# A recurrent layer on one core: the decay of each step computed as a power of 1 + exp(v) on Pool, instead of as a power of two from the softplus

## The chip, the cores and the metric

The kernel runs as one program on one core of a Trainium2 chip. The metric is the time of one execution on the device, in microseconds (us). Before the change it is 4870.85 us, the median of 3 runs (4870.28 to 4872.86). Engines are named as in the profile: PE does matrix products, PEld loads their weights, DVE is the vector engine, ACT the one for activation functions, POOL (Pool) the general one, SP issues DMAs.

## The reference

The whole network has four layers, each an attention-like part and a feed-forward part. Only the first part of layer 0 is touched, a recurrence over 512 steps for 8 sequences. It cannot be computed in parallel over the steps, because the output of a step enters the projections of the next one:

```
def step(carry, inp):
    state, y_prev = carry
    xBC_t, dt_t, z_t = inp
    xBC = silu(xBC_t + y_prev @ W_rxbc.T)
    dtr = silu(dt_t + y_prev @ W_rdt.T)
    x_t, Bv, Cv = xBC[:, :256], xBC[:, 256:384], xBC[:, 384:]
    dt = softplus(dtr + dt_bias)
    dA = exp(dt * A)                                   # A = -exp(A_log), one for each of 4 heads
    state = state * dA + dt * x_h * Bv                 # 8 x 4 heads x 64 x 128
    y = (state * Cv).sum(-1) + D * x_h
    g = y * silu(z_t)
    yn = g * rsqrt(mean(g * g) + EPS) * norm_w
    return (state, yn), yn @ W_out.T
```

A head has 64 of the 256 inner channels. The step needs dt (how much of the new input enters the state) and dA (how much of the old state stays), one number of each for a head and a sequence.

## The kernel before, in words

`layer0` holds the loop. It is written with a manual schedule: each engine gets its instructions in the order of the program text, so the order of the lines is the order of the work on each engine. Engines wait for each other through semaphores.

The state is not updated in every step. `S` holds the state as of a multiple of eight steps (`Q = 8`), and the steps since then are kept as a list in `xw` (dt times x, already decayed to the present) beside their B rows in `h`. `held(t)` says which multiple is in use at step t, and `past` is the number of listed steps, 5 to 12. Every eight steps `update` folds the older entries into the next `S`, spread over the steps t mod 8 = 0 to 4 (its parts are called through `part(t, place)`). `spans` gives the columns of the ring of 16 entries that a step has to touch; with more than eight entries they are in two pieces.

Layout: 128 partitions are four groups of 32, with the 8 sequences in the first rows of each group for what is in rows, and the channels over the partitions for what is transposed. The DVE transpose works within blocks of 32 x 32, and carries data between the two. Before the change two heads stand in each partition group (the channels are in two halves of 128, and a half holds two heads), so dt is a tile of two columns, and dt and its decay need one transpose each.

A step goes like this, by the line numbers of the profile. PE squares the last step's output for its norm (L216, `pym`) and multiplies it with the recurrent weights (L216, `pag`). DVE sums the squares (L271, `ms`), Pool makes the power -1/2 (L274, `rh`), DVE scales the projections and adds the precomputed rows (L308, `a`), and ACT takes the silu (L314, `ar`), followed by a table load for the softplus (L211). DVE transposes (L316, `h`) and multiplies the listed B rows with C (L331, `cb`); PE sums these over the state dimension (L338, `G` in `pag`) and multiplies C (laid out by Pool in `Z`, L322) with the held state (L345, `py` in `pym`). ACT takes the softplus (L352, `dt`). DVE forms the weighted sum of the list (L358 `tmp`, L366 `R`), the exponent of the decay (L372), and Pool the power of two of it (L373, `da`). DVE turns dt, `py` and da (L255: `td`, `ty`, `dA`), and puts the output together: the share of the held state (L395, `y`), of the list (L386 and L401, `R`), both decayed (L408), and of the step itself (`M`, L383, L396, L406); their sum is `yh` (L409), on which PE waits for the next step. After that DVE decays the list (L418) for the next step.

Beside this the loop carries a second stream: the experts of layer 0's feed-forward part (`ffn.products` on PE, `ffn.activate` on ACT, `ffn.add` on DVE, a few in each step) and the projections of later steps (`aside`). `occupy` issues products of an identity matrix, whose results nobody reads, to fill PE where neither stream has work. `tables` loads ACT's table set, twice a step.

In the built program, where an instruction has to wait for two semaphores, an EventSemaphore instruction on the same engine stands ahead of it and waits for the first of them; the profile lists L308's, for instance, as 639 of 21 ns each.

Of the kernel before, what the change touches and what calls it, by code (L numbers as in the profile page):

```python
# [56 lines left out]
RW = 130  # L57
# [3 lines left out]
ASIDE = {5: 0, 7: 1, 13: 2, 15: 3, 9: 4}  # L61
LAG = 5


class Projections:
# [4 lines left out]
    def __init__(self, tc, ctx, K, I, dr, xn, xnT, B, T):  # L70
# [6 lines left out]
        self.WdtT = wp.tile([P, 8], F32, name="WdtT")  # L77
# [7 lines left out]
        with ExitStack() as c2:  # L85
# [9 lines left out]
            for c in range(2):  # L95
# [5 lines left out]
                self.dt(c, pz[:, 256:264])  # L101
                self.send(c, pz[:, 256:264])
# [19 lines left out]
    def send(self, c, ps):  # L122
        stg = self.stg.pop(c)
        self.nc.vector.tensor_copy(stg[:, :, P:RW], ps.rearrange("p (j c) -> p j c", j=4))
        self.pd[c] = self.dr.tile([4, TC, self.B, RW], F32, name=f"pd{c}")
        self.nc.sync.dma_start(out=self.pd[c].rearrange("j t b f -> (t b) j f"), in_=stg)
# [10 lines left out]
def layer0(tc, K, I, dr, xn, s_all, s_out, x, B, T):  # L137
# [12 lines left out]
    with ExitStack() as ctx:  # L150
# [18 lines left out]
        dtb = load("dtb", [P, 2])  # L169
        Dp = load("Dp", [P, 2, B])  # L170
        A2 = load("Al", [P, 2])
        selj = load("selj", [P, 2, P])
        nc.scalar.activation(A2, A2, AF.Exp)
        nc.vector.tensor_scalar(A2, A2, -1.0 / math.log(2.0), None, ALU.mult)
        two = wp.tile([P, 2], F32, name="two")
        nc.vector.memset(two, 2.0)
        for k in range(2):
            nc.vector.tensor_scalar(Wr[:, k], Wr[:, k], nw[:, k : k + 1], None, ALU.mult)
            nc.vector.tensor_scalar(WoT[:, k], WoT[:, k], nw[:, k : k + 1], None, ALU.mult)
        half = wp.tile([P, 1], F32, name="half")  # L180
# [21 lines left out]
        pdt, ring = paside[:, 256:264], [paside[:, 0:P], paside[:, P : 2 * P]]  # L202
# [58 lines left out]
        def pair(name):  # L261
            return wk.tile([P, 2], F32, name=name)
# [30 lines left out]
        def step(t, rt, zt):  # L293
# [26 lines left out]
            v, dt = pair("v"), pair("dt")  # L320
            nc.gpsimd.tensor_tensor(v, ar[:, P:RW], dtb, ALU.add)
            nc.gpsimd.tensor_copy(bass.AP(z9.tensor, z9.offset, [list(z9.ap[0]), [9, B]]), C)  # L322
            zd, xz, xd = small("zd"), small("xz"), small("xd")
            nc.gpsimd.tensor_tensor(zd, xw[:, :, :, SINCE[held(t) % 2]], zt, ALU.mult)
            nc.gpsimd.tensor_tensor(xz, x, zt, ALU.mult)
            nc.gpsimd.tensor_tensor(xd, xz, Dp, ALU.mult)
# [3 lines left out]
            for lo, hi in spans(t, t + 1):  # L330
# [5 lines left out]
                o += hi - lo  # L336
            for j in range(4):
# [14 lines left out]
            nc.scalar.activation(dt, v, AF.Softplus)  # L352
# [10 lines left out]

            def total(c):
                if past:
                    nc.vector.tensor_reduce(out=R[:, c, :], in_=tmp[:, c, :, 0:past], op=ALU.add, axis=AX.X)  # L366


            da, long = pair("da"), past > Q

            def power():
                tt_(da, dt, A2, ALU.mult)  # L372
                nc.gpsimd.tensor_tensor(da, two, da, ALU.pow)  # L373

            if long:
                power()
            total(0)
            total(1)
            if not long:
                power()  # L380
            td = turned(dt.unsqueeze(2).to_broadcast([P, 2, 32]), 2, "td")[:, :, 0:B]
            M = small("M")
            tt_(M, xz, G[:, :, past].unsqueeze(1).to_broadcast([P, 2, B]), ALU.mult)  # L383
            occupy(5 - given, pag[:, 384:])
            if past:
                tt_(R, R, zt, ALU.mult)  # L386
            part(t, "copies")
            if t % Q:
                ffn.activate(1 if t % TC in (9, 10) else 2 if t % TC in (3, 7, 11, 15) else 3)
            tables(SILU)  # L390
            nc.gpsimd.tensor_tensor(xw[:, :, :, s + 1], td, x, ALU.mult)
            part(t, "half 1")
            ty = turned(py.rearrange("p (c e) -> p c e", e=32), 2, "ty")
            y = small("y")
            tt_(y, zd, ty[:, :, 0:B], ALU.mult)  # L395
            tt_(M, M, td, ALU.mult)  # L396
            turn = lambda: turned(da.unsqueeze(2).to_broadcast([P, 2, 32]), 2, "dA")[:, :, 0:B]
            if long:
                dA = turn()
            if past:  # L400
                tt_(R, R, y, ALU.add)  # L401
            else:
                R = y
            if not long:
                dA = turn()
            tt_(M, M, xd, ALU.add)  # L406

            tt_(R, R, dA, ALU.mult)  # L408
            tt_(yh[:, :, :, t], R, M, ALU.add)  # L409

# [6 lines left out]
            for lo, hi in todo:  # L417
                tt_(xw[:, :, :, lo:hi], xw[:, :, :, lo:hi], dA.unsqueeze(3).to_broadcast([P, 2, B, hi - lo]), ALU.mult)  # L418
            if t % Q == 0:
                nc.vector.tensor_copy(xw[:, :, :, SINCE[n % 2]], dA)  # L420

        def update(q):
# [4 lines left out]
            das = st.tile([P, 2, 4, 4], F32, name="das")  # L427
            bs = st.tile([P, 2, P], F32, name="bs")
# [7 lines left out]

            def turn():
                xT = psU.tile([P, 2, 2, P], F32, name="xT", tag="u")
                both = psU.tile([P, 512], F32, name="bT", tag="u")
                bT = both[:, 0 : 2 * P].rearrange("p (r k) -> p r k", r=2)  # L440
                da = both[:, 2 * P : 2 * P + 4 * B].rearrange("p (c j b) -> p c j b", c=2, j=2)
# [1128 lines left out]
```

## Time and profile before

| | |
|---|---|
| median of 3 runs | 4870.85 us |
| profiled execution | 4871.46 us |
| its span | 4869.7 us |
| loop of layer 0, first to last L314 | 117.7 to 2902.1 us, 2784.4 us |
| busy in the loop: PE, DVE, ACT, POOL | 2694, 2111, 2221, 1384 us |
| granted PE clock in the loop | 1.00 of full |

The page of the profile has six parts. The second shows how the engines' load lies over the span, in 40 slices of about 122 us each, in tenths:

```profile
PE   6999999999999999999999997869999897999998
DVE  4777777777777777777777775747777325777771
ACT  2787788777787777887788773436666224666665
POOL 1455445444455444554544552620000345777782
```

The loop is the even stretch of some 23 slices from the second one on. PE looks full there, and DVE and ACT are busy for some three quarters of the time. None of these shares says what a step waits for, because PE's includes the filling products. That is read from the timeline and the chain of waits inside single steps. In a line of the timeline the columns are: start in us, duration in us, engine, line, operation, what is written and read, the shapes, the count, and in brackets how long the engine had been idle and what ended that. In a line of the groups of instructions they are: line, engine, operation, names, shapes, count, then busy time in all and the mean in ns, then idle time before and its releasers.

### The profile page before, as it was taken

Reading aid. Unit: us, or ns where it says so; the run is one execution under the profiler, and the core shown is the slowest. Engines: PE = TensorE matmul, PEld = TensorE weight load, DVE = VectorE, ACT = ScalarE, POOL = GpSimd, SP = SyncE. Lnnn points to the kernel's source line nnn. Section 1 sums busy time; section 2 is a strip of 40 time slices with the busy share of each in tenths; the row PEclk is TensorE's granted clock in tenths of the full one; section 3 lists DMA queues with packets and bytes.
Section 4 is the critical chain, followed back from the end, with each engine's and each line's share of the span. In section 5 each row is a group of like instructions: output and inputs, shape, how many; then the busy total and the mean of one; then the engine's idle time right before and its main releaser. Section 6 shows DMA issues by size and latency. Waiting matters only on the chain.

```text
span 4869.7 us, 193476 instructions
## 1 busy us (share of the span) xinstructions
PE 4555.9 (94%) x80433; PEld 3410.4 (70%) x80433; DVE 3393.6 (70%) x16561; ACT 3297.6 (68%) x6513; POOL 2241.9 (46%) x5416
## 2 busy tenths in 40 slices
PE   6999999999999999999999997869999897999998
PEld 5888888788877888788887885325555554666666
DVE  4777777777777777777777775747777325777771
ACT  2787788777787777887788773436666224666665
POOL 1455445444455444554544552620000345777782
PEclk6999999999999999999999998769999898999999
DMA  3000000000000000000000003100000510000000
GB/s 96 8 9 15 9 11 12 9 11 13 9 10 13 11 9 13 10 9 15 9 9 10 9 26 74 43 0 2 2 2 2 106 36 20 2 2 2 2 2 18
DMA packets 72706, 81.68 MB, mean 17 GB/s; under 512 B 8716, under 2 KB 55056, under 8 KB 71698
## 3 DMA queue, kind: packets, MB, share of 16 engines
q1 hardware_dynamic: 67116, 65.31, 5.5%
q8 instruction: 631, 10.34, 0.9%
q10 hardware_dynamic: 4710, 3.99, 0.3%
q14 instruction: 249, 2.04, 0.1%
HBM read 52.92 MB, written 16.36 MB: 14 GB/s over the span
## 4 chain that ended last, share of the span: by engine, by line
PE 54%; DVE 28%; POOL 7%; ACT 7%; issue 4%; DMA 1%; SPq 0%; DVEq 0%; ACTq 0%; POOLq 0%
PE pt L949 7%; PE ps_s L928 4%; PE pym L216 4%; POOL rh L274 4%; PE pym L221 3%; PE pag L338 3%; PE po L963 3%; PE pym L345 3%; PE ph L663 3%; PE us L468 3%; DVE a L308 2%; DVE R L366 2%; ACT ar L314 2%; DVE tmp L358 2%; DVE h L316 2%
## 5 line engine op out<-in xcount | busy, mean ns | idle before, releaser
L211 ACT ACT_TABLE_LOAD x1024 | 1313.8, 1283 | 17.7
L274 POOL TENSOR_TENSOR rh<-ms,half 128x1 f32<-128x1 f32 x512 | 281.3, 549 | 751.6 <-DVE ms L271 751.6
L345 PE MATMUL pym<-S,Z 128*8 128x64 f32 x32768 | 552.0, 219 | 0.2
L1247 POOL TENSOR_SCALAR gp<-toe,ng 128x207 f32<-128x207 f32 (+1 forms) x512 | 490.0, 965 | 111.2 <-DVE mn L936 75.9
L314 ACT ACTIVATE ar<-a 128x130 f32<-128x130 f32 x511 | 159.7, 313 | 534.4 <-DVE a L308 534.2
L949 PE MATMUL pt<-ident,sb 128*128 128x128 f32 x3328 | 498.7, 284 | 13.2 <-ACT pT L952 8.5
L949 PEld LDWEIGHTS pt<-ident,sb 128*128 128x128 f32 x3328 | 357.4, 141 | 209.6 <-ACT pT L954 78.6
L345 PEld LDWEIGHTS pym<-S,Z 128*8 128x8 f32 x32768 | 489.5, 90 | 0.9 <-POOL Z L322 0.8
L373 POOL TENSOR_TENSOR da<-two,da 128x2 f32<-128x2 f32 x512 | 356.8, 697 | 241.8 <-DVE da L372 241.8
L221 PE MATMUL pym<-ones,ident 128*128 128x128 f32 x3378 | 466.1, 277 | 0.0
L952 ACT COPY pT<-pt 128x512 f32<-128x512 f32 (+3 forms) x512 | 255.5, 499 | 245.0 <-PE pt L949 243.6
L221 PEld LDWEIGHTS pym<-ones,ident 128*128 128x128 f32 x3378 | 418.4, 192 | 0.7 <-DVE ms L271 0.4
L936 DVE CUSTOM_DVE_ANT_0 sb<-ps_s,gp 128x512 f32<-128x512 f32 x512 | 324.1, 685 | 102.8 <-PE ps_s L928 85.3
L216 PE MATMUL pag<-w_Wr,yh 128*8 128x130 f32 x8176 | 353.4, 278 | 0.0
L942 ACT ACTIVATE sb<-sb,mn 128x512 f32<-128x512 f32 (+3 forms) x512 | 330.6, 646 | 22.1 <-DVE mn L936 16.6
L358 DVE TENSOR_TENSOR tmp<-xw,pag 128x176 f32<-128x176 f32 (+2 forms) x635 | 159.8, 268 | 236.6 <-PE pag L338 236.6
L663 PE MATMUL ph<-xhT,ew 128*128 128x128 f32 x2048 | 315.8, 292 | 0.0
L308 DVE SCALAR_TENSOR_TENSOR a<-pag,rh,rows 128x130 f32<-128x130 f32 x511 | 180.6, 353 | 193.7 <-POOL rh L274 193.4
L485 ACT ACTIVATE Sd<-S,das 128x64 f32<-128x64 f32 x1008 | 306.1, 404 | 3.0
L673 ACT ACTIVATE hid<-ph,be 128x128 f32<-128x128 f32 x1024 | 305.8, 357 | 1.1 <-PE ph L663 1.1
L663 PEld LDWEIGHTS ph<-xhT,ew 128*128 128x128 f32 x2048 | 253.8, 191 | 70.0 <-issue 64.5
L646 PE MATMUL po<-ew,hid 128*128 128x128 f32 x2048 | 296.5, 288 | 6.0
(360 smaller groups left out, 10292.7 us busy)
## 6 DMA issues: line engine op xcount, KB each, us to landing
cB<-dc SPq DMA_DIRECT2D x16, 1024.0 KB
pd<-stg SPq DMA_DIRECT2D x32, 260.0 KB
rows<-pd SPq DMA_DIRECT2D x256, 32.5 KB
wu<-in_f_up_dram SPq DMA_DIRECT2D x9, 512.0 KB
wd<-in_f_down_dram SPq DMA_DIRECT2D x9, 512.0 KB
rd<-rv SPq DMA_DIRECT2D x1, 3304.0 KB
x<-in_u_dram SPq DMA_DIRECT2D x8, 256.0 KB
w<-in_f_w_dram SPq DMA_DIRECT2D x8, 256.0 KB
```

Source lines behind the costliest of these rows:

```text
L211: nc.scalar.preload_act_table_set(name)
L216: nc.tensor.matmul(out[32 * j : 32 * j + B, :], lhsT, rhs(j), start=(k == 0), stop=(k == 1))
L221: nc.tensor.matmul(where, ident, K["ones"], start=True, stop=True)
L274: nc.gpsimd.tensor_tensor(rh[:, t : t + 1], ms, half, ALU.pow)
L345: nc.tensor.matmul(py[32 * j : 32 * j + B, :], z9[:, B * b : B * b + B], Sq[b % 4][:, b // 4, :, 32 * j : 32 * j + 32], start=(i == 0), st ...
L373: nc.gpsimd.tensor_tensor(da, two, da, ALU.pow)
L485: nc.scalar.activation(Sd[:, 1, k, :], So[i][:, 1, k // 2, 64 * (k % 2) : 64 * (k % 2) + 64], AF.Copy, scale=das[:, 1, k, i : i + 1],)
L663: self.nc.tensor.matmul(self.ph[:, f, :], self.w[n][0][:, f * P : (f + 1) * P], self.xhT[:, i * P : (i + 1) * P], start=True, stop=True)
L936: nc.vector.tensor_tensor_reduce(out=sb[:, 0:L], in0=ps[:, g, 0:L], in1=bias[g], scale=1.0, scalar=3.0e38, op0=ALU.add, op1=ALU.min, accum ...
L942: nc.scalar.activation(sb[:, 0:L], sb[:, 0:L], AF.Exp, scale=-1.0, bias=mn)
L949: nc.tensor.transpose(pt[:, j * P : (j + 1) * P], sb[:, j * P : (j + 1) * P], self.ident)
L1247: nc.gpsimd.tensor_scalar(t[:, k0:k1], toe[:, h, o : o + k1 - k0], gates[b][:, i, h : h + 1], None, ALU.mult)
```

## The change

In the reference dA = exp(A softplus(v)) with v = dtr + dt_bias. Since softplus(v) = ln(1 + exp(v)), this is (1 + exp(v)) to the power A. The change computes it in that form. v is capped at 40 in the exponential; beyond that, the exponent is scaled by v/40 instead (`Acap`, `ad`).

- Decay: Pool computes min(v, 40), then Euler's number to that power (`base` holds it), plus one, and then the power `ad`, four dependent instructions from `ar` on. The softplus for dt stays on ACT and takes the bias itself. dt and the decay go into the two columns of one tile `dd`, which one transpose turns.
- Layout: each of the four partition groups holds one head. The channels are reordered in `layout` (`by_head`), so a half holds 32 channels of each head, dt has one column instead of two, and the rows of the projections have 129 columns for 130 (`RW`).
- Order: Z's copy, xz and the two small instructions for `ad` go to DVE, ahead of `tmp`. `za` (gate times decay), the product of M with dt and its sum with xd go to Pool, behind the transpose. y is multiplied with `za` once, in place of three products on DVE. In steps with `past` above 8 the transpose stands between the two reduces; else there is one reduce for both halves.
- The update of S every eight steps takes its decays through `decays`, a Pool product with a 0/1 mask `firsts`, and one product on PE, instead of two on PE with `selj`.
- ACT's ReLUs of the experts follow the table `RELUS` by t mod 8, and one filling product less is issued behind the held state's products.

```diff
-RW = 130
+RW = 129
+CAP = 40.0
+RELUS = [2, 1, 1, 1, 2, 4, 4, 3]
...
-            v, dt = pair("v"), pair("dt")
-            nc.gpsimd.tensor_tensor(v, ar[:, P:RW], dtb, ALU.add)
-            nc.gpsimd.tensor_copy(bass.AP(z9.tensor, z9.offset, [list(z9.ap[0]), [9, B]]), C)
-            zd, xz, xd = small("zd"), small("xz"), small("xd")
-            nc.gpsimd.tensor_tensor(zd, xw[:, :, :, SINCE[held(t) % 2]], zt, ALU.mult)
-            nc.gpsimd.tensor_tensor(xz, x, zt, ALU.mult)
-            nc.gpsimd.tensor_tensor(xd, xz, Dp, ALU.mult)
+            d, ad = ar[:, P:RW], one_("ad")
+            dd = wk.tile([P, 2], F32, name="dd")
+            e, w = one_("e"), one_("w")
+            nc.gpsimd.tensor_scalar(e, d, dtb, CAP, ALU.add, ALU.min)
+            nc.gpsimd.tensor_tensor(e, base, e, ALU.pow)
+            nc.gpsimd.tensor_tensor(e, e, one, ALU.add)
...
+            nc.vector.tensor_copy(bass.AP(z9.tensor, z9.offset, [list(z9.ap[0]), [9, B]]), C)
+            nc.vector.tensor_scalar(w, d, dtb, Acap, ALU.add, ALU.mult)
+            xz, xd = small("xz"), small("xd")
+            tt_(xz, x, zt, ALU.mult)
+            nc.vector.tensor_scalar(ad, w, A, None, ALU.min)
+            nc.gpsimd.tensor_tensor(dd[:, 1:2], e, ad, ALU.pow)
...
-            nc.scalar.activation(dt, v, AF.Softplus)
+            nc.scalar.activation(dd[:, 0:1], d, AF.Softplus, bias=dtb)
...
-            def power():
-                tt_(da, dt, A2, ALU.mult)
-                nc.gpsimd.tensor_tensor(da, two, da, ALU.pow)
...
+            M = small("M")
+            own = lambda: tt_(M, xz, both(G[:, :, past]), ALU.mult)
+            nc.gpsimd.tensor_tensor(xd, xz, Dp, ALU.mult)
+            turn = lambda: turned(dd.unsqueeze(2).to_broadcast([P, 2, 32]), 2, "td")
+            if past > Q:
+                nc.vector.tensor_reduce(out=R[:, 0, :], in_=tmp[:, 0, :, 0:past], op=ALU.add, axis=AX.X)
+                own()
+                turns = turn()
+                nc.vector.tensor_reduce(out=R[:, 1, :], in_=tmp[:, 1, :, 0:past], op=ALU.add, axis=AX.X)
+            else:
...
+                    nc.vector.tensor_reduce(out=R, in_=tmp[:, :, :, 0:past], op=ALU.add, axis=AX.X)
+                own()
+                turns = turn()
+            td, dA = both(turns[:, 0, 0:B]), turns[:, 1, 0:B]
+            occupy(4 - given, pag[:, 384:])
...
-            if t % Q:
-                ffn.activate(1 if t % TC in (9, 10) else 2 if t % TC in (3, 7, 11, 15) else 3)
+            ffn.activate(RELUS[t % Q])
...
+            za = small("za")
+            nc.gpsimd.tensor_tensor(za, zt, both(dA), ALU.mult)
+            nc.gpsimd.tensor_tensor(M, M, td, ALU.mult)
+            nc.gpsimd.tensor_tensor(M, M, xd, ALU.add)
             nc.gpsimd.tensor_tensor(xw[:, :, :, s + 1], td, x, ALU.mult)
...
-            tt_(y, zd, ty[:, :, 0:B], ALU.mult)
-            tt_(M, M, td, ALU.mult)
...
-            tt_(M, M, xd, ALU.add)
-            tt_(R, R, dA, ALU.mult)
-            tt_(yh[:, :, :, t], R, M, ALU.add)
+            tt_(y, xw[:, :, :, SINCE[held(t) % 2]], ty[:, :, 0:B], ALU.mult)
+            if past:
+                tt_(y, y, R, ALU.add)
+            tt_(y, y, za, ALU.mult)
+            tt_(yh[:, :, :, t], y, M, ALU.add)
...
+            def spread():
+                nc.gpsimd.tensor_tensor(
+                    decays, xw[:, 0, :, SINCE[q % 2]].unsqueeze(1).to_broadcast([P, 4, B]),
+                    firsts.unsqueeze(2).to_broadcast([P, 4, B]), ALU.mult,
+                )
...
-                for j in range(2):
-                    nc.tensor.matmul(
-                        da[:, :, j, :], selj[:, j, :], xw[:, :, :, SINCE[q % 2]], start=True, stop=True
-                    )
+                nc.tensor.matmul(da, K["ones"], decays, start=True, stop=True)
```

## The prediction

> **What bounds the kernel now.** I read the page first, then the chain of waits inside one step of the layer 0 loop, then the timeline of that step, then the same places over all steps. The page gives a span of 4869.7 us. The loop of 512 steps lies from the first L314 at 117.7 us to the last at 2902.1 us: 2784.4 us, 5.44 us a step. Nothing in the diff touches what comes after the loop. The timeline of one step (L314 starts at 1502.40; rows between are left out):
>
> ```profile
> 1502.40 0.31 ACT L314 ACTIVATE ar<-a 128x130 f32<-128x130 f32 x1 [1.43 <-DVE a L308]
> ...
> 1502.79 0.20 POOL L321 TENSOR_TENSOR v<-ar,w_dtb 128x2 f32<-128x2 f32 x1 [0.81 <-ACT ar L314]
> ...
> 1503.74 0.26 DVE L358 TENSOR_TENSOR tmp<-xw,pag 128x96 f32<-128x96 f32 x1 [0.43 <-PE pag L338]
> ...
> 1504.03 0.20 ACT L352 ACTIVATE dt<-v 128x2 f32<-128x2 f32 x1
> 1504.03 0.31 DVE L366 TENSOR_REDUCE R<-tmp 128x8 f32<-128x48 f32 x2
> ...
> 1504.51 0.70 POOL L373 TENSOR_TENSOR da<-two,da 128x2 f32<-128x2 f32 x1 [0.46 <-DVE da L372]
> ...
> 1504.56 0.17 DVE L386 TENSOR_TENSOR R<-R,z 128x16 f32<-128x16 f32 x1
> 1504.65 0.24 DVE L255 STREAM_TRANSPOSE ty<-pym 128x64 f32<-128x64 f32 x1
> 1504.92 0.17 DVE L395 TENSOR_TENSOR y<-zd,ty 128x16 f32<-128x16 f32 x1
> ...
> 1505.24 0.25 DVE L255 STREAM_TRANSPOSE dA<-da 128x64 f32<-128x64 f32 x1
> ...
> 1505.52 0.17 DVE L408 TENSOR_TENSOR R<-R,dA 128x16 f32<-128x16 f32 x1
> 1505.73 0.19 DVE L409 TENSOR_TENSOR yh<-R,M 128x16 f32<-128x16 f32 x1
> ```
>
> PE is busy 94% of the span, but much of that is the identity products that only fill time. The chain of waits runs L314, h, cb, PE L338, tmp, R, then DVE instruction after DVE instruction up to yh (L409), then PE, ms, rh, a (L308) and the next L314. From yh's start to the next L314 it is 1.96 to 1.99 us and nothing in the change lies on it. So **a step moves by as much as the start of yh moves against its own L314.** Call that distance Y, and count all times below from L314's start. Over all steps the trace has Y = 3.32 (t mod 8 = 5, 6), 3.36 (7), 3.45 (0), 3.55 (1 to 3), 3.58 (4): mean 3.46.
>
> What decides Y now: softplus (ACT, 1.63 to 1.83, right behind the 1.28 us table load), then DVE's da, then the Pool power of 0.70, 2.11 to 2.81, then dA's transpose and two dependent sums. DVE itself has almost no hole from 1.63 on.
>
> **What the change does to it.**
>
> *The decay leaves the softplus.* New Pool chain from ar: e (tensor_scalar 128x1), base^e, e+1, e^ad. Start 0.39, where v starts now. A dependent Pool instruction begins 0.08 after its predecessor's end (xz ends 1503.747, xd starts 1503.825). The power of one element has a row, the plus one is nearest to v's 0.195. The tensor_scalar has no small row. The groups kept apart by shape give
>
> ```profile
> L274 POOL TENSOR_TENSOR rh<-ms,half 128x1 f32<-128x1 f32 x512 | 281.3, 549 | 751.6 <-DVE ms L271 751.6
> L1247 POOL TENSOR_SCALAR gp<-toe,ng 128x286 f32<-128x286 f32 x256 | 270.4, 1064 | 57.7 <-DVE mn L936 57.7
> L1247 POOL TENSOR_SCALAR gp<-toe,ng 128x207 f32<-128x207 f32 x256 | 219.6, 866 | 53.5 <-issue 23.3 <-DVE mn L936 18.3 <-DVE ng L1208 11.1
> ```
>
> The medians of the two L1247 forms are 813 and 1009 ns, so 2.48 ns an element and 0.30 us at none. Below, v's 0.195 (a plain sum) bounds it; above, 0.30 + 0.195 = 0.50. I take **0.30**, since it comes from the same opcode with the same kind of operand. Then e 0.39 to 0.69, base^e 0.77 to 1.32, plus one 1.40 to 1.59, e^ad 1.67 to 2.22. DVE sees a Pool result 0.03 later (da's end to dA): **both are turned at T = 2.25**, where dA's transpose started at 2.83 to 3.04 before. Softplus is done at 1.83 as now and does not decide. This is the one new wait on DVE: behind it on that engine stand ty, y and all that leads to yh (in long steps the second reduce too), and PE's next products wait for yh.
>
> *DVE's row after T.* Two transposes follow each other by 0.16 (td to M now). So ty at T+0.16, lasting 0.24; y 0.03 behind its end, at T+0.43, 0.175 long; the sum with R 0.035 behind that, T+0.64 to T+0.82. The last two wait for DVE and Pool. The built program puts the DVE wait into an EventSemaphore of its own ahead of the instruction (three more a step on DVE). What that costs shows where it is there now, in layer 1 (timeline of DVE):
>
> ```profile
> 3122.28 1.24 DVE L807 TENSOR_SCALAR cp<-cp,ar,k 128x512 f32<-128x512 f32 x1 [0.46 <-ACT cp L806]
> 3123.62 0.69 DVE L810 TENSOR_TENSOR cp<-cp,pw 128x512 f32<-128x512 f32 x1
> ```
>
> L807 ends at 3123.51 and L810 starts 0.104 later (0.039, the semaphore instruction's 0.021, 0.044) instead of 0.034. So y*za runs from T+0.92 to T+1.10 and yh starts at **T+1.20**. In the long steps (t mod 8 = 1 to 4, over eight past values) the second reduce stands between the transposes: 0.15 more, T+1.35.
>
> *The sums on Pool* are cover, not path: za starts 0.08 behind the transposes' end, T+0.32; M*td 0.18 later; M+xd waits for it, T+0.81 to T+1.03; seen at T+1.06, ahead of y*za's end by only 0.04. xw follows, over before L419. If a Pool product were 0.1 us longer, M would decide.
>
> *Moved onto DVE ahead of tmp:* Z's copy, w, xz, ad, about 0.1 each. They fit into the 0.43 hole between cb and tmp, and tmp still waits for PE L338; Z is ready about when Pool had it (0.95 against 0.99). Were the hole gone, tmp could slip 0.1 before R's end would reach T. *Gone from DVE:* da, R*z, M*td, M+xd, one transpose, one reduce in short steps. Worth nothing alone: DVE now waits for T.
>
> *The rest costs nothing:* the long decay of S (0.62 on Pool) still runs between rh and e, with 0.2 us to spare; decays (128x32) runs between xw and rh; ACT has the ReLUs moved to the steps without the four L493 copies, and its second table load ends by 4.5 where the next L314 comes at 5.3; 478 of 2193 filling products go, all in front of PE's wait for yh; no DMA of the loop moves, rows and pd carry one column less in 130.
>
> **Sum.** With T = 2.25, Y becomes 3.45 in short steps and 3.60 in long ones. Against the trace: +0.13, +0.13, +0.09, 0.00, +0.05 three times, +0.02: 0.52 in eight steps, 0.065 a step, times 512 = **33 us slower**. The profiled execution took 4871.46 us (1.8 outside its span), the median shown is 4870.85: 4904.
>
> **Two rules against the trace.** The Trainium skill, *SBUF — State Buffer*, "Who interferes with whom": a DVE instruction with two SBUF inputs is locked out by a Pool instruction that reads SBUF[...]. Here R*z (L386, two SBUF inputs) starts 0.05 us into the 0.70 us power and takes its usual 0.17; only an instruction that starts within some 0.03 us of a Pool product loses anything (y, L395: 0.23 instead of 0.175 where xw on Pool starts just ahead of it). By the row the overlap costs nothing, by the rule Z's copy or y would sit out a power or a product: 0.1 to 0.3 us a step, 50 to 150 us. I take the row. *GPSIMD Engine Reference*, "Engine selection", speaks against moving two-input products to Pool (about twice the time). The row is 0.22 against 0.175. By the rule M would be ready at T+1.45 rather than T+1.06, another 0.25 a step, 128 us.
>
> **Rivals.**
> 1. *Forecast, 0.53*: the Pool chain sets T at about 2.25 and two semaphore instructions follow; 4904, own range 4880 to 4945.
> 2. *Faster, 0.28*: the tensor_scalar costs what a plain sum does. T = 2.15, Y falls by 0.04 on average, 4851. It decides from a price under 0.235, where the 0.065 is used up. For it: the fit is drawn from 207 elements down to one. Against: two forms and the 512 elements of L585 (1.57 us) lie on one line. If the semaphore instructions also slid under the running instruction (2 x 0.07), it would be 4833 with the larger price.
> 3. *Contention, 0.12*: the lock of the rule, about 5000. For it: y's 0.23. Against: L386.
> 4. *PE's clock, 0.07*: fewer filling products and 0.3 us more idling in front of yh lower the granted clock, now 1.00 over the whole loop; a tenth of the 2 us of PE work on the chain would be 0.2 a step, 4970.
>
> **How the numbers follow.** Time 4904. The low end takes in rival 2 and part of its second half, 4840; the high end takes the upper price only in part (0.50 would give +0.265 a step, 5006) and most of 4: 4975. A measurement of this kernel tells 0.2% (10 us) from no change. Faster: rival 2 but for its small cases, and a few of 1: 0.28. Within: 0.07. Slower: 0.65.
>
> **What would show it.** e's row on Pool at 0.30 and the start of the two-column transpose at 2.25 after L323 (the new number of L314); a gap of 0.10 in front of y*za and of yh; M+xd on Pool ending just before y*za. If e is under 0.24, or those gaps are 0.03, the sign turns. If the distance from yh to the next L323 changes, my claim that nothing else moves is wrong.

## The result, and the profile after

| | before | after |
|---|---|---|
| median | 4870.57 us (4868.89 to 4872.86, 4 runs) | 4916.23 us (4915.33 to 4929.06, 4 runs) |
| profiled execution, its span | 4871.46, 4869.7 us | 4929.06, 4926.9 us |
| loop, first to last silu (L314, now L323) | 2784.4 us | 2828.7 us |

The ratio is 1.010 (95% interval 1.0082 to 1.0117): the kernel became 46 us slower. The profiled execution is the slowest of the four; some 12 us of its excess lie behind the loop, 10 of them in layers 2 and 3, which the change doesn't touch, and the other three runs, at 4915 to 4916, are shorter by about as much. The loop's own 44 us, and its start 1 us later, make up 45 of the 46.

The second part of the page, three of its rows after the change (each digit the busy share of a fortieth of the span, in tenths; PEclk the granted TensorE clock):

```profile
PE   6988888888888888888888897869999897999998
...
POOL 1666666666666666666666662630000355767782
PEclk6999999999999999999999998769999898999999
```

PE went from nine tenths to eight in the loop, because the filling products went; Pool went from four or five to six; the clock stays at nine and more, and in the loop it is 1.00 as before. Rival 4, a lower clock, fell with this row.

The fourth part, the chain of work that ended last, by engine and by line:

```profile
PE 35%; DVE 25%; POOL 25%; issue 8%; ACT 6%; DMA 1%; DVEq 0%; SPq 0%; ACTq 0%; POOLq 0%
PE pt L955 7%; POOL rh L283 6%; POOL dd L351 5%; PE ps_s L934 4%; POOL e L334 4%; DVE a L317 4%; PE pym L221 3%; ACT ar L323 3%; PE po L969 3%; DVE td L260 2%; POOL e L333 2%; DVE yh L410 2%; DVE y L409 2%; DVE xw L419 2%; PE py L1122 2%
```

Before, the first row was:

```profile
PE 54%; DVE 28%; POOL 7%; ACT 7%; issue 4%; DMA 1%; SPq 0%; DVEq 0%; ACTq 0%; POOLq 0%
```

Pool's new instructions, e and dd, are on the chain now, and so is the transpose behind them. The power no longer waits for ACT, and hardly for DVE, but DVE waits for it.

The timeline of one step with t mod 8 = 6 (start in us, duration, engine, line, operation, names; in brackets the idle time before and what ended it). Its silu starts at 1568.90:

```profile
1568.90 0.31 ACT L323 ACTIVATE ar<-a 128x129 f32<-128x129 f32 x1 [1.70 <-DVE a L317]
...
1569.31 0.29 POOL L333 TENSOR_SCALAR e<-ar,w_dtb 128x1 f32<-128x1 f32 x1 [0.83 <-ACT ar L323]
...
1569.69 0.56 POOL L334 TENSOR_TENSOR e<-base,e 128x1 f32<-128x1 f32 x1
...
1570.59 0.55 POOL L351 TENSOR_TENSOR dd<-e,ad 128x1 f32<-128x1 f32 x1
...
1571.17 0.24 DVE L260 STREAM_TRANSPOSE td<-dd 128x64 f32<-128x64 f32 x1 [0.32 <-POOL dd L351]
1571.34 0.21 DVE L260 STREAM_TRANSPOSE ty<-pym 128x64 f32<-128x64 f32 x1
...
1571.59 0.18 DVE L406 TENSOR_TENSOR y<-xw,ty 128x16 f32<-128x16 f32 x1
...
1571.80 0.18 DVE L408 TENSOR_TENSOR y<-y,R 128x16 f32<-128x16 f32 x1
...
1571.98 0.22 POOL L400 TENSOR_TENSOR M<-M,xd 128x16 f32<-128x16 f32 x1
1572.08 0.17 DVE L409 TENSOR_TENSOR y<-y,za 128x16 f32<-128x16 f32 x1
...
1572.36 0.19 DVE L410 TENSOR_TENSOR yh<-y,M 128x16 f32<-128x16 f32 x1
```

Four Pool instructions (the third, e+1, lies between the rows shown) run one behind the other from 0.41 to 2.24 after the silu. DVE stands idle for 0.32 until the last has ended, and turns at 2.27. From there to yh it is 1.19. In the step shown before, dA's transpose came much later (1505.24, 2.84 after its silu), but only 0.49 lay between it and yh. So the decay is ready 0.57 earlier and yh still starts 0.13 later: what was done while DVE waited for the decay (turning `py`, forming `y`, adding `R`, multiplying M) now stands behind that wait.

The groups of Pool's instructions kept apart by shape (busy time in all, mean ns of one, idle time before and its releasers):

```profile
L334 POOL TENSOR_TENSOR e<-base,e 128x1 f32<-128x1 f32 x512 | 286.0, 559 | 42.6
...
L351 POOL TENSOR_TENSOR dd<-e,ad 128x1 f32<-128x1 f32 x512 | 280.3, 548 | 42.3 <-DVE tmp L373 2.0 <-POOL e L335 0.5 <-DVE ad L350 0.4
...
L333 POOL TENSOR_SCALAR e<-ar,w_dtb 128x1 f32<-128x1 f32 x512 | 149.5, 292 | 281.9 <-ACT ar L323 281.9
...
L335 POOL TENSOR_TENSOR e<-e,ones 128x1 f32<-128x1 f32 x512 | 97.3, 190 | 40.2
```

292 ns for the tensor_scalar against 190 for the plain sum is the price on which the prediction hung its sign. The idle time of 42 us over 512 steps, 0.08 each, in front of the dependent instructions is the gap that the prediction took from xz and xd.

### The profile page after: what moved, and what is told of

Same layout as the page of the kernel before. It is cut to its first block, busy times and chain, and to the rows that moved or that the text cites. A ratio compares the mean times of both kernels' runs of the same rounds, so it can differ in the third digit from the quotient of the medians.

```text
span 4926.9 us, 193651 instructions
## 1 busy us (share of the span) xinstructions
PE 4406.9 (89%) x79351; PEld 3282.5 (67%) x79351; DVE 3473.6 (71%) x15792; ACT 3346.8 (68%) x6513; POOL 2623.5 (53%) x6503
## 3 DMA queue, kind: packets, MB, share of 16 engines
q14 instruction: 267, 2.19, 0.2%
## 4 chain that ended last, share of the span: by engine, by line
PE 35%; DVE 25%; POOL 25%; issue 8%; ACT 6%; DMA 1%; DVEq 0%; SPq 0%; ACTq 0%; POOLq 0%
PE pt L955 7%; POOL rh L283 6%; POOL dd L351 5%; PE ps_s L934 4%; POOL e L334 4%; DVE a L317 4%; PE pym L221 3%; ACT ar L323 3%; PE po L969 3%; DVE td L260 2%; POOL e L333 2%; DVE yh L410 2%; DVE y L409 2%; DVE xw L419 2%; PE py L1122 2%
## 5 line engine op out<-in xcount | busy, mean ns | idle before, releaser
L323 ACT ACTIVATE ar<-a 128x129 f32<-128x129 f32 x511 | 159.7, 312 | 521.3 <-DVE a L317 521.1
L221 PE MATMUL pym<-yh 128*8 128x8 f32 x8192 | 231.7, 219 | 223.0 <-DVE yh L410 222.7
L226 PE MATMUL pym<-ones,ident 128*128 128x128 f32 x2942 | 417.6, 277 | 0.0
L221 PEld LDWEIGHTS pym<-yh 128*8 128x8 f32 x8192 | 173.5, 154 | 361.8 <-DVE yh L410 357.6
L226 PEld LDWEIGHTS pym<-ones,ident 128*128 128x128 f32 x2942 | 369.7, 192 | 0.4 <-DVE ms L280 0.4
L221 PE MATMUL pag<-w_Wr,yh 128*8 128x129 f32 x8176 | 352.7, 277 | 0.0
L317 DVE SCALAR_TENSOR_TENSOR a<-pag,rh,rows 128x129 f32<-128x129 f32 x511 | 180.6, 353 | 197.9 <-POOL rh L283 195.3
L334 POOL TENSOR_TENSOR e<-base,e 128x1 f32<-128x1 f32 x512 | 286.0, 559 | 42.6
L351 POOL TENSOR_TENSOR dd<-e,ad 128x1 f32<-128x1 f32 x512 | 280.3, 548 | 42.3 <-DVE tmp L373 2.0
```

Of the source, the lines that this page charges most:

```text
L221: nc.tensor.matmul(out[32 * j : 32 * j + B, :], lhsT, rhs(j), start=(k == 0), stop=(k == 1))
L226: nc.tensor.matmul(where, ident, K["ones"], start=True, stop=True)
L317: stt_(a, pa, rh[:, t - 1 : t], rt, ALU.mult, ALU.add)
L334: nc.gpsimd.tensor_tensor(e, base, e, ALU.pow)
L351: nc.gpsimd.tensor_tensor(dd[:, 1:2], e, ad, ALU.pow)
```

## The experiments

Y is, as in the prediction, the start of yh counted from the step's own silu, and T the start of the two-column transpose; both are medians by t mod 8 without the first 16 steps, averaged over the eight where one number is given. Short steps are those with t mod 8 = 0 and 5 to 7, long ones those with 1 to 4. A change of Y by 0.02 is worth 10 us. My theory: the loss is the price of e, plus a row behind T that is longer by two waits for two semaphores, with M on Pool only just hidden. Against it stood that DVE and Pool get in each other's way (the lock), that the shifted filling products and ReLUs cost the time, and that the layout itself is at fault.

| run | time, us | ratio to before (95%) | mean Y, us | step, us |
|---|---|---|---|---|
| before | 4870.57 | | 3.460 | 5.443 |
| after | 4916.23 | 1.010 (1.0082 to 1.0117) | 3.544 | 5.518 |
| e1: plain sum for e | 4882.84 | 1.0026 (1.0017 to 1.0035) | 3.473 | 5.448 |
| e2: M's sums on DVE | 4888.99 | 1.0040 (1.0023 to 1.0057) | 3.470 | 5.451 |
| e3: all three sums on DVE | 4913.66 | 1.0086 (1.0068 to 1.0104) | 3.519 | 5.497 |
| e4: layout alone | 4846.54 | 0.9948 (0.993 to 0.9965) | 3.391 | 5.389 |
| e5: `py` turned first | 4894.06 | 1.0049 (1.0033 to 1.0064) | 3.509 | 5.486 |
| e6: one more Pool product | 4935.2 | 1.0119 (1.0091 to 1.0147) | 3.572 | 5.548 |
| e7: old filling and ReLUs | 4918.64 | 1.0096 (1.0074 to 1.0118) | 3.551 | 5.527 |
| e8: no cap, row reordered | 4786.72 | 0.9820 (0.9799 to 0.9842) | 3.268 | 5.276 |
| e9: e8's row, with the cap | 4836.73 | 0.9936 (0.9914 to 0.9958) | 3.367 | 5.372 |

The times before in the sessions were 4868.7 (e1 to e4), 4871.66 (e5 to e8) and 4867.55 us (e9). All of e1 to e9 start from the changed kernel.

### e1: what the tensor_scalar costs

```diff
-            nc.gpsimd.tensor_scalar(e, d, dtb, CAP, ALU.add, ALU.min)
+            nc.gpsimd.tensor_tensor(e, d, dtb, ALU.add)
```

It leaves out the cap of v at 40 in the exponential.

> The changed kernel, with e formed by a plain Pool sum (v = d + dtb) instead of the tensor_scalar; the cap at 40 is left out. Theory (the Pool chain sets the start T of the two-column transpose): e takes 0.195 instead of 0.29, T goes from 2.27 to about 2.18, the step loses 0.09, 512 steps lose 48 us: about 4868, level with the kernel before. Rival (something else holds the transpose, softplus or DVE's own row): no change, 4916.

e took 0.190 and started 0.02 earlier (0.390), which alone would bring everything behind it 0.12 earlier, but T moved only from 2.276 to 2.201: by 0.11 to 0.13 where t mod 8 is 5 to 7, by 0.03 to 0.07 in the other steps. Why not further, its group on Pool shows:

```profile
L351 POOL TENSOR_TENSOR dd<-e,ad 128x1 f32<-128x1 f32 x512 | 280.8, 549 | 70.0 <-DVE ad L350 29.7 <-DVE tmp L373 3.5
L334 POOL TENSOR_TENSOR e<-base,e 128x1 f32<-128x1 f32 x512 | 280.7, 548 | 40.1
```

The idle time before the last power rose from 42.3 to 70.0 us, and 29.7 of it are now ended by DVE's `ad`, which the changed kernel's row names with 0.4. A wait that nothing had shown stood right behind the one removed. Y fell by 0.071, 36 us; the times differ by 33. The term is real and large, but not the whole loss: against before, 0.26% remain.

### e2: M's two sums back on DVE

```diff
-            nc.gpsimd.tensor_tensor(M, M, td, ALU.mult)
-            nc.gpsimd.tensor_tensor(M, M, xd, ALU.add)
...
             tt_(y, xw[:, :, :, SINCE[held(t) % 2]], ty[:, :, 0:B], ALU.mult)
+            tt_(M, M, td, ALU.mult)
             if past:
                 tt_(y, y, R, ALU.add)
+            tt_(M, M, xd, ALU.add)
             tt_(y, y, za, ALU.mult)
```

> The changed kernel, with the two sums of M (times td, plus xd) back on DVE, between y, the sum with R and the product with za. yh then waits for DVE alone, without a semaphore instruction ahead of it. Theory (each semaphore instruction that waits for the instruction just before it costs 0.07, and the gaps between dependent DVE instructions have room for independent ones): the gap in front of yh falls from 0.10 to 0.03, 36 us less, about 4880. Rival (two more DVE instructions on the row cost what they last, 0.09 each): 4916 or more, up to 5000.

Two more instructions on the engine that leads to yh made the kernel 0.6% faster. The timeline of DVE in the step corresponding to the one above (silu at 1548.62):

```profile
1551.30 0.18 DVE L404 TENSOR_TENSOR y<-xw,ty 128x16 f32<-128x16 f32 x1
1551.40 0.17 DVE L405 TENSOR_TENSOR M<-M,td 128x16 f32<-128x16 f32 x1
1551.52 0.17 DVE L407 TENSOR_TENSOR y<-y,R 128x16 f32<-128x16 f32 x1
1551.67 0.17 DVE L408 TENSOR_TENSOR M<-M,xd 128x16 f32<-128x16 f32 x1
1551.80 0.17 DVE L409 TENSOR_TENSOR y<-y,za 128x16 f32<-128x16 f32 x1
1552.01 0.19 DVE L410 TENSOR_TENSOR yh<-y,M 128x16 f32<-128x16 f32 x1
```

From y to y*za it takes 0.50, against 0.49 in the changed kernel without the two in between. An instruction that does not depend on the one ahead of it starts some 0.08 before that one's recorded end, as M's product with td does here (M's sum with xd, which has a semaphore of Pool to wait for, only 0.02), so the links of a chain of dependent sums leave room for one such instruction each. What is gained is behind y*za: yh starts 0.04 after its end (1551.97) instead of 0.11, because it no longer waits for Pool. That is the price of the second semaphore, 0.07 a step, 36 us; mean Y fell by 0.074, and the times differ by 27. It is not that Pool was late: in the changed kernel the gap ahead of y*za is the same 0.104, though za was done 0.25 and more before y+R ended. Nor did the program lose an EventSemaphore instruction: yh's stands ahead of M's sum with xd now, where the chain has room for it.

The Trainium skill, *GPSIMD Engine Reference*, "Engine selection", speaks against two-input sums on Pool for their duration, about twice that on DVE. Here they last 0.22 against 0.17, 1.3 times as long, and as long as they are hidden that duration is not what was paid: the wait at the meeting point was.

### e3: all sums behind the transpose on DVE

Besides e2's edit, `za` goes to DVE:

```diff
-            nc.gpsimd.tensor_tensor(za, zt, both(dA), ALU.mult)
...
             tt_(y, xw[:, :, :, SINCE[held(t) % 2]], ty[:, :, 0:B], ALU.mult)
+            tt_(za, zt, both(dA), ALU.mult)
+            tt_(M, M, td, ALU.mult)
```

> As e2_m_on_dve, with za on DVE too, so none of the sums behind the transpose is on Pool (xd and the product for the list stay there). The product with za then has no semaphore instruction (0.07 less), but three independent instructions stand between y and the sum with R, one too many for the gap (0.06 more). Theory: level with e2 within 30 us, 4880 to 4910. If Pool products held DVE up through the shared access to the memory, this one would be clearly the fastest of the two, below 4860.

With only one Pool product left beside DVE's row the kernel was no faster than e2 but slower by 0.5%. The row in the step with t mod 8 = 6:

```profile
1565.57 0.18 DVE L403 TENSOR_TENSOR y<-xw,ty 128x16 f32<-128x16 f32 x1
...
1565.83 0.17 DVE L407 TENSOR_TENSOR y<-y,R 128x16 f32<-128x16 f32 x1
1566.02 0.17 DVE L408 TENSOR_TENSOR M<-M,xd 128x16 f32<-128x16 f32 x1
1566.11 0.17 DVE L409 TENSOR_TENSOR y<-y,za 128x16 f32<-128x16 f32 x1
```

From y to y+R it takes 0.26 where e2 has 0.22, since two instructions stand in one link, where there is room for one. That is the whole difference between the two in mean Y (0.049). The 0.07 that the expectation counted for the semaphore ahead of y*za did not come: from y+R to y*za it is 0.28 in both, because M's sum with xd, which still waits for Pool, now starts only 0.02 behind y+R's end. In e8, where xd is on DVE too, it is 0.21.

Rival 3 is the Trainium skill's rule (*SBUF — State Buffer*, "Who interferes with whom": a DVE instruction with two SBUF inputs contends with a Pool instruction that reads SBUF, and the lock is exclusive). e3 alone can't rule it out, since the fuller link could hide a gain; the durations can. The traces have the lock, but it is short. A DVE sum of 128x16 that starts up to 0.07 behind the start of a Pool product of that size ends 0.243 to 0.249 after the Pool product's start, whenever in that time it began (the prediction had put the reach at 0.03): y in the long steps of the changed kernel (0.182 to 0.205, 0.066 to 0.043 behind M's product with td), y before (up to 0.234) and here where t mod 8 = 0 (0.228), R+y in e4. One that starts later than that (y in short steps, 0.18), or just ahead of the Pool product (y+R, 0.175), is not longer. So a Pool product holds DVE up as if for the first 0.07 of its 0.22 and no longer, at most 0.06 of delay. In the changed kernel that is 0.03 in the worst step, where rival 3 counted some 0.25 in each. It fell.

### e4: the layout without the new order

Layer 0's step in the old order, with the old softplus and power of two, on one head to a partition group; what stays of the change is `by_head`, `RW` and `decays`:

```diff
-            nc.gpsimd.tensor_scalar(e, d, dtb, CAP, ALU.add, ALU.min)
...
-            nc.gpsimd.tensor_tensor(dd[:, 1:2], e, ad, ALU.pow)
+            nc.gpsimd.tensor_tensor(v, ar[:, P:RW], dtb, ALU.add)
...
+                tt_(da, dt, A2, ALU.mult)
+                nc.gpsimd.tensor_tensor(da, two, da, ALU.pow)
```

> One head a partition group, as in the changed kernel, but the step itself in the order of the kernel before: softplus, exponent on DVE, power of two on Pool, two transposes, sums on DVE. Theory: the power has one element instead of two (0.55 instead of 0.70) and the transposes are half as wide; DVE's row is nearly full, so only 0.07 to 0.12 of the 0.15 reaches yh: 36 to 61 us below the kernel before, 4810 to 4835. Rival (DVE's row alone bounds the step): 4870.

The layout alone is a gain of 0.5%, smaller than expected. What became shorter is the power, on one column instead of two, in the group of Pool's instructions:

```profile
L379 POOL TENSOR_TENSOR da<-two,da 128x1 f32<-128x1 f32 x512 | 292.6, 572 | 240.3 <-DVE da L378 240.3
```

572 ns where before had 697; dt's and dA's transposes fell from 0.24 to 0.205. In long steps yh came 0.07 to 0.12 earlier. The shortfall is in the short ones, on DVE: dA's transpose starts where it did (2.836 against 2.832), though the power ended 0.10 earlier, and R+y (0.175 before) took 0.19 to 0.226, because xw on Pool starts just ahead of it. Of the 0.069 that Y gained, 0.015 was lost again behind yh, half of it where t mod 16 = 9 and the period stayed at 5.63. So the change as a whole is two things of opposite sign: 24 us won by the layout, 70 lost by the new decay and the new order together.

### e5: the held state's share turned ahead of the decay

```diff
+            ty = turned(py.rearrange("p (c e) -> p c e", e=32), 2, "ty")
+            turns = turn()
```

in place of the two in the opposite order, and both reduces ahead of them.

> The changed kernel with one change of order on DVE: ty (which needs only PE's py, ready at about 2.2 in short steps and 2.35 in long ones) is turned ahead of dt and decay, and both reduces stand ahead of the transposes. M stays on Pool. Theory (the sums of M on Pool are hidden by no more than 0.04, as the prediction had it): y starts 0.17 to 0.3 earlier, but the two-column transpose moves back to 2.36 and 2.51, M follows it by 1.06, and yh now waits for Pool: 3.42 and 3.58, some 0.04 a step, about 4896. Rival (M is well hidden, DVE's chain behind ty decides): 0.17 a step, 4830.

The time came out within 2 us of the expectation. The timeline of DVE's row and Pool's M at t mod 8 = 6 (silu at 1555.40):

```profile
1557.63 0.25 DVE L260 STREAM_TRANSPOSE ty<-pym 128x64 f32<-128x64 f32 x1 [0.27 <-PE pym L360]
...
1558.44 0.17 DVE L406 TENSOR_TENSOR y<-y,za 128x16 f32<-128x16 f32 x1
1558.56 0.22 POOL L398 TENSOR_TENSOR M<-M,xd 128x16 f32<-128x16 f32 x1
...
1558.81 0.19 DVE L407 TENSOR_TENSOR yh<-y,M 128x16 f32<-128x16 f32 x1 [0.20 <-POOL M L398]
```

y*za ends at 1558.61, 0.14 earlier than in the changed kernel (counted from the silu), and then yh waits 0.20 for M from Pool. Here the bracket names a releaser, where the changed kernel's row had none: the cover of M was used up. What the order wins in y is lost in M, and mean Y falls by 0.035 only.

### e6: how thin M's cover is

```diff
+            nc.gpsimd.tensor_tensor(junk, zt, both(dA), ALU.mult)
             nc.gpsimd.tensor_tensor(M, M, td, ALU.mult)
```

> The changed kernel with one further Pool product of 128x16 (its result is not read) between za and M's first sum. Theory: M is 0.18 later; in short steps its cover is 0.13, counted to the start of yh, so yh moves by 0.05; in long steps the cover is 0.3 and nothing moves: 14 us more, about 4930. Rival 1 (all of Pool's work behind the transpose is on the path): 0.18 a step, 5008. Rival 2 (hidden everywhere): 4916.

As expected: one product more, spaced by 0.18, moved yh by 0.06 in short steps and not at all in long ones. So M had 0.12 to 0.13 to spare to yh's start in the short steps, and more in the long ones.

### e7: the old filling products and ReLUs

```diff
-            occupy(4 - given, pag[:, 384:])
+            occupy(5 - given, pag[:, 384:])
...
-            ffn.activate(RELUS[t % Q])
+            if t % Q:
+                ffn.activate(1 if t % TC in (9, 10) else 2 if t % TC in (3, 7, 11, 15) else 3)
```

> The changed kernel with the filling products and the ReLUs' distribution of the kernel before. Theory: neither is on the path, the granted clock is full in the loop with and without them: no change, 4916 within 10. Rival (fewer filling products cost clock): 4880 or less.

No change (4918.64 against 4916.23, intervals overlapping almost whole). The filling and ACT's part of the change give nothing, and cost too little for the time to show. The traces show 2 us: in the changed kernel, and in every run with its ReLU table, the steps t = 489 and 505 near the loop's end are 1.0 longer than others of their kind; before, in e4 and in e7, which have the old ReLUs, they are not. The first of them on ACT:

```profile
2826.32 0.40 ACT L679 ACTIVATE hid<-ph,be 128x128 f32<-128x128 f32 x1 [2.04 <-PE ph L669]
...
2829.00 0.29 ACT L323 ACTIVATE ar<-a 128x129 f32<-128x129 f32 x1
```

A ReLU waits 2.04 for PE's product, the table load of 1.28 and the four copies of 1.06 follow, and the silu starts 1.08 after its input `a` was ready (2827.92) instead of 0.03.

### e8 and e9: everything that the runs had shown, in one order

e8 takes e1's plain sum (so it leaves out the cap, and with it w and ad: the exponent is A), puts both reduces ahead of the transpose, and fills the links of DVE's chain one by one: za between ty and y, M's first sum between y and y+R, its second between y+R and y*za. xd goes to DVE ahead of `tmp`.

```diff
-            nc.gpsimd.tensor_scalar(e, d, dtb, CAP, ALU.add, ALU.min)
+            nc.gpsimd.tensor_tensor(e, d, dtb, ALU.add)
...
-            nc.gpsimd.tensor_tensor(dd[:, 1:2], e, ad, ALU.pow)
+            nc.gpsimd.tensor_tensor(dd[:, 1:2], e, A, ALU.pow)
...
             ty = turned(py.rearrange("p (c e) -> p c e", e=32), 2, "ty")
+            tt_(za, zt, both(dA), ALU.mult)
             tt_(y, xw[:, :, :, SINCE[held(t) % 2]], ty[:, :, 0:B], ALU.mult)
+            tt_(M, M, td, ALU.mult)
             if past:
                 tt_(y, y, R, ALU.add)
+            tt_(M, M, xd, ALU.add)
             tt_(y, y, za, ALU.mult)
```

> What the readings point to, in one kernel: e as a plain sum, the power taken with the constant exponent (so w and ad go and the last power waits for Pool alone; the cap at 40 is left out), xd in DVE's hole ahead of tmp, both reduces ahead of the transpose, za in the hole between ty's issue and its end, M's sums between y and R, no semaphore instruction behind the transpose. Theory: transpose at 2.14 in short and about 2.2 to 2.3 in long steps, yh 1.03 to 1.06 behind it: Y about 3.24 on average against 3.46 before and 3.54 in the changed kernel: about 4760. Rival (DVE's own row bounds the step, as e3 is level with the changed kernel): 4870 to 4916.

T came at 2.141 in short steps and Y at 3.268: 1.8% under before, though 27 us over the expectation. e9 keeps the cap, with e, w, ad and xd where the changed kernel has them, and takes only the order of the row. It computes what the changed kernel does:

> The order of the run before (both reduces ahead of the transpose, za and M's sums on DVE between ty, y and the sums), but with the cap of the changed kernel kept: e by the tensor_scalar on Pool, w and ad on DVE, xd on Pool behind the power. So it computes what the changed kernel does. If the start of the transpose and then the row behind it set yh, the transpose comes at 2.28 in short steps (2.14 without the cap) and 2.30 to 2.40 in long ones, yh at 3.32 to 3.45, mean about 3.37, period 5.38, time 4835 to 4850: under both kernels. The rival theory, that the gain of the run before came from leaving out the cap and not from the order, expects 4880 or more. The other rival, that in that run PE's queue and not yh was the bound, expects less than 20 us between the two runs.

4836.73 us, 0.64% under before and 79 us under the changed kernel, with T at 2.26 to 2.39 and mean Y at 3.367, as expected. The order without the missing cap is thus worth 79 us. e8's further 50 come with leaving out the cap and with xd on DVE together; no run separates these. Against e4 (0.9948, e9 0.9936) the intervals overlap: with the cap, the new decay in its best order here gives no more than the layout alone, as far as these runs can tell. The row in the step with t mod 8 = 6 (silu at 1523.66):

```profile
1525.94 0.24 DVE L260 STREAM_TRANSPOSE td<-dd 128x64 f32<-128x64 f32 x1 [0.32 <-POOL dd L351]
1526.11 0.21 DVE L260 STREAM_TRANSPOSE ty<-pym 128x64 f32<-128x64 f32 x1
1526.24 0.15 DVE L400 TENSOR_TENSOR za<-z,td 128x16 f32<-128x16 f32 x1
...
1526.81 0.17 DVE L406 TENSOR_TENSOR y<-y,za 128x16 f32<-128x16 f32 x1
1527.01 0.19 DVE L407 TENSOR_TENSOR yh<-y,M 128x16 f32<-128x16 f32 x1
```

The same wait of 0.32, the same transpose as in the changed kernel, and yh 1.07 behind it instead of 1.19, with three instructions more on DVE.

What is next in line shows where t mod 16 = 9. There the period is 5.59 in e9, although yh starts as early as in its neighbours (3.34). DVE in such a step:

```profile
1542.99 0.19 DVE L407 TENSOR_TENSOR yh<-y,M 128x16 f32<-128x16 f32 x1
...
1544.02 0.17 DVE L280 CUSTOM_DVE_ANT_0 own<-pym,w_diag 128x8 f32<-128x8 f32 x1 [0.52 <-PE pym L221]
```

The sum of squares comes 1.03 behind yh, where it comes 0.75 behind it in other steps, and waits for PE. PE's timeline says with what PE was busy:

```profile
1542.86 0.71 PE L131 MATMUL paside<-s,WinT 128*128 128x128 f32 x4
1543.50 0.43 PE L221 MATMUL pym<-yh 128*8 128x8 f32 x15
```

yh is done at 1543.18, and the products with it start at 1543.50, behind four projections of a later step that share this step with the update of S. In the changed kernel yh came 0.28 later in these steps, and the sum of squares 0.76 behind it, without that wait. So in one step of sixteen PE's queue has become the bound (in the kernel before it held there too, by 0.10). It costs 0.27 in 32 steps of e9, 9 us; in e8, where the same steps stand at 5.60 between neighbours at 5.21, it costs 12 of the 27 us by which that run missed its expectation. The rest is in Y, 3.268 instead of 3.24: T in the long steps was at 2.19 to 2.34, where 2.2 to 2.3 had been expected, and where t mod 8 = 0 yh came 1.12 behind T instead of 1.04. For t mod 8 = 2 to 4 DVE has no idle time ahead of the transpose in e8 (0.07 to 0.12 in the changed kernel), so there its own row and no longer Pool's chain sets T.

## Why the prediction was right

Direction and mechanism were right, and the size was short by 12 us of 46. By its steps:

| step of the prediction | forecast | measured |
|---|---|---|
| start of e on Pool | 0.39 | 0.410 |
| e by tensor_scalar | 0.30 | 0.292 |
| T, the two-column transpose, short steps | 2.25 | 2.261 to 2.274 |
| T, long steps | 2.25 | 2.266 to 2.302 |
| from T to yh, short steps | 1.20 | 1.183 |
| from T to yh, long steps | 1.35 | 1.350 to 1.354 |
| gap ahead of y*za and yh, by the second semaphore | 0.104 | 0.104 |
| M+xd seen ahead of y*za's end by, short steps | 0.04 | 0.03 |
| Y in short steps | 3.45 | 3.444 to 3.457 |
| Y in long steps | 3.60 | 3.619 to 3.656 |
| from yh to the next silu | unchanged, 1.96 to 1.99 | 1.974 (before 1.983) |

**The mechanism.** The four-instruction chain on Pool sets T, and what follows it is longer than what followed dA. e1 and e2 each took away one of the two costs that the prediction named (the tensor_scalar's price, the wait for a second semaphore) and got back 33 and 27 us. Neither alone reached the time before: the lower ends of their intervals, 1.0017 and 1.0023, stay above 1.

**The term that was mis-sized** is T in the long steps: 0.02 to 0.05 later than the 2.25 that the sum used for all steps. 0.02 of it is the start of e, at 0.410 where v and e1's plain sum start at 0.39. The rest is mostly the first power, which takes 559 ns on average, 547 to 575 by t mod 8, where rh's row has 549; in e1, where it runs 0.13 us earlier, it takes 548. What lengthens it was not tried. Y came out 0.02 to 0.06 above 3.60, nearly all of it from T. By the medians the eight steps sum to 0.67 instead of 0.52: 0.084 a step, 43 us instead of 33. Of this, 0.009 a step (5 us) came back between yh and the next silu. The last 6 of the loop's 44 us are not in the medians: 2 are the two ReLU steps of e7's account, a part of the change that the prediction put at nothing, and in the profiled execution single steps are 0.15 to 0.35 longer, and one near the loop's end (t = 491) 0.8, where the granted clock was 0.76 to 0.90 (2830 to 2840 us). What causes these last was not tried.

**Where the numbers met by luck.** The row behind T took the forecast 1.35 in long steps because two small errors cancel: y starts 0.01 to 0.04 earlier behind T than was counted, and y (0.182 to 0.205 instead of 0.175) and y*za (0.184) last longer beside Pool's products. In short steps the later T was made good by a row of 1.18 instead of 1.20, since ty took 0.21 and not 0.24.

**The rivals.** 2 (the tensor_scalar as cheap as a plain sum) fell with the row of 292 ns. It would not have brought 4851 either, nor turned the sign: e1 is that case, and gave 4882.84, because ad on DVE then holds the power where t mod 8 is 0 to 4. The prediction had costed w and ad at about 0.1 each and taken them to be hidden. w lasts 0.266, and ad, which needs it, another 0.214 (the groups of DVE's instructions in the changed kernel, by shape); the exponent was only just ready. With Z's copy and xz they filled DVE's hole ahead of `tmp` to the last (0.42 to 0.51 of idle time before, none after), which T, still later, hid. 3 (the lock) fell with the durations given under e3, 4 (the clock) with the clock's row. One of the two gaps at 0.03 doesn't turn the sign either (e2); with both gone, and the sums in the links, it turned (e9).

```profile
L347 DVE TENSOR_SCALAR w<-ar,w_dtb,Acap 128x1 f32<-128x1 f32 x512 | 136.1, 266 | 0.0
...
L350 DVE TENSOR_SCALAR ad<-w,w_Al 128x1 f32<-128x1 f32 x512 | 109.5, 214 | 0.0
L410 DVE TENSOR_TENSOR yh<-y,M 128x16 f32<-128x16 f32 x512 | 96.2, 188 | 55.6 <-POOL xw L401 2.0 <-DVE y L409 1.2
L406 DVE TENSOR_TENSOR y<-xw,ty 128x16 f32<-128x16 f32 x512 | 95.8, 187 | 17.8
L409 DVE TENSOR_TENSOR y<-y,za 128x16 f32<-128x16 f32 x512 | 92.0, 180 | 54.0 <-POOL xw L401 0.9
```

The rows of yh and y*za show the two semaphores over the whole loop: 55.6 and 54.0 us of idle time, 0.11 a step each, where y and y+R have 17.8 and 17.6 (0.035). Almost none of it has a releaser in the profile, since by the semaphores nothing was late.

**What the prediction didn't see** is that the layout is a gain by itself (e4), so that the new decay and the order of the step cost 70 and not 46 us, and that the three sums have room between DVE's dependent ones.

## What to carry to other kernels

When a slow value is made ready earlier, count what has to follow it: work that used to fill the wait, and now stands behind it, is added to the path in full. The short chain of dependent sums on DVE had room for one independent instruction in each link here, so a sum moved to another engine to relieve DVE may save nothing there and cost a wait where the two meet. A gap in front of an instruction to which the profile gives no releaser is worth comparing with its neighbours': here it was 0.11 instead of 0.035 in every step, and taking one of the two away gave back 27 of the 46 us.

## What was not expected of the hardware

- A tensor_scalar on one column is dearer here than a sum over sixteen: on DVE 266 ns with two one-column operands (`dtb`, `Acap`) and 214 with one (`A`), against 155 to 180 for most 128x16 tensor_tensors; on Pool 292 against 190 for a one-column tensor_tensor.
- The softplus on ACT took 295 ns on one column with the bias as an operand, and 204 without it, on two columns (before) and on one (e4). It is not on the path here.
- A Pool power costs 548 to 572 ns on average on one column and 697 on two.
- An instruction on DVE that does not depend on the one ahead starts some 0.08 before that one's recorded end, a dependent one 0.035 behind it. So the recorded duration of 0.17 is not what one more instruction costs: in e8 it takes 0.43 from y to y*za with two of them in between, which is what the two dependent sums and their gaps last alone.
- A Pool product of 0.22 holds up a DVE sum with two inputs only if the sum starts within 0.07 of it, and then until 0.25 after the product's start (under e3). Beside a Pool power of 0.70 (before, R*z starting 0.05 into it) nothing of the kind shows: 0.166.
